# Queries and keys turned in blocks of 32 by 32 on VectorE and put in place by transfers through DRAM

## The chip, the cores and the metric

The kernel runs on one core of one Trainium2 chip. The metric is the device time of one execution in microseconds (us); the figure compared is the median of several runs. The profile is one execution taken by the hardware profiler. Its engines are PE (TensorE, with PEld for its weight loads), DVE (VectorE), ACT (ScalarE), POOL (GpSimd) and SP (SyncE, which here issues every transfer).

## What is computed

The input `x` is 8 sequences of 512 tokens with 256 features, all float32. It is normalised, and two branches read it. The first is causal attention with one head of 256 features. The second is a stack of two layers of windowed attention (8 heads of 64 features, windows of 128 tokens that also see the window before) and a gated feed-forward network. The output is `x + s * silu(g)`, with `s` from the first branch and `g` from the second.

What matters for this change is in the second branch, cut from the reference:

```python
qkv = h @ wqkv
q, k, v = jnp.split(qkv, 3, axis=-1)
q, k, v = (to_heads(q), to_heads(k), to_heads(v))
q = l2norm(q) * qs
k = l2norm(k) * ksc
q, k = rotary_xpos(q, k)
...
sim = jnp.einsum('bhwid,bhwjd->bhwij', bq, bk)
```

The product `sim` sums over the 64 features of a head. TensorE sums over partitions, so queries and keys are needed with features on partitions, while normalisation and rotation are done with tokens on partitions. Between the two, each tile of 128 tokens by 512 features has to be turned.

## The kernel before

Work is cut into slots, one for each pair of a sequence `b` and a layer `l`, in the order (0,0), (1,0), (0,1), (2,0), (1,1) and so on: 16 slots. A slot has four tiles `t` of 128 tokens; `steps` is the list of all 64 tiles. A set of generators describes the work, each yielding before a piece of TensorE work the events, buffers and PSUM banks that it needs:

- `start` loads and normalises a sequence, turns it, and runs the first branch (`qk0`, `sc0`, `pT0p`, `av0`).
- `project` multiplies a tile by the weights (`qkv`, for keys, queries and values in turn). ACT squares the result into `sq`; VectorE makes the two rotary products `r` and `side` and the sum of squares `ss`; POOL adds `side` to `r`, raises `ss` to the power -0.5 (`rn`) and multiplies `r` by it. The finished `r` is 128 tokens by 512 features.
- `turns` turns each `r`: four TensorE transposes of 128 by 128 into a PSUM bank (`qkT`), then one copy on ACT or VectorE to `qT` or `kT`, laid out as [feature within the chunk, chunk of 128 features, token].
- `all_scores` multiplies queries and keys (`sps`) on quarters of TensorE's array, 64 by 64, then masks, takes the exponent and divides. `all_turns` turns the weights (`pTp`, `pTr`), `all_sums` weighs the values (`ops`, also on quarters), and `all_outs` projects (`wop`).
- `feed_forward` does the normalisation and the network (`hps`, `hT`, `ff`, `w2p`), and `finish` the gate and the output.

`projections` keeps at most two tiles ahead of the scores. Buffers are limited by `counts`: two `qT`, three `kT`, eight `r`.

The class `Order` plans while the program is written: it keeps an account of time for TensorE, ready times of events and buffers, and a table of ranks (with the offsets in `SHIFT`) by which it chooses the next piece. TensorE executes the pieces in the order chosen. Work of VectorE, ACT and POOL is entered in each engine's own time line through `order.on`, and that fixes the order on these engines. SP is not planned: its transfers stand in the order that the framework's scheduler gives them. `STAY` is the rank by which the planner prefers to stay in the present shape of the array.

Of the kernel before, what the change touches and what calls it, by code (L numbers as in the profile page):

```python
# [14 lines left out]
P = 128  # L15
# [23 lines left out]


SHIFT = {
    "causal": {2: 1.5, 4: 1.5, 6: 1.5},
    "finish": {4: 2.75},
    "forward": {2: 1, 3: -0.5, 5: 0.25, 6: 0.75, 7: -0.25, 8: 1, 10: 1, 12: 1, 13: -0.25, 15: -0.25, 16: 1},
    "hold": {1: 4, 7: 12, 8: 12, 9: 1, 12: 24},
    "out": {4: -2, 14: 0.75},
    "project": {1: -0.25, 3: -0.5, 5: -0.5, 6: -0.5, 11: 0.5, 13: 0.75},
    "scores": {15: -2.0},
    "sum": {3: -0.75, 4: -1, 5: 0.25, 7: -0.75, 9: -0.75, 11: -0.5, 12: -0.25, 13: -0.75, 14: 1},
    "turn": {5: -0.5, 8: 0.5},  # L50
    "weigh": {0: 0.25, 2: 0.5, 3: 1, 8: 0.25, 9: 0.25, 11: 1.0, 12: -0.75, 14: 0.25},
}


# [16 lines left out]
class Order:  # L71
# [16 lines left out]
    HOLD = 2.0  # L88


    STAY = 2.0
    TURNS = 0.0

    PATIENCE = 0.0
    HOP = 0.15
    TABLE = 1.3

    LATE = {"DVE": 0.085, "ACT": 0.11, "POOL": 0.03}

    def __init__(self, tc, buffers):  # L100
        self.now = 0.0
        self.idle = 0.0
        self.shape = None
        self.changes = 0
        self.free = {tag: [0.0] * n for tag, n in buffers.items()}
        self.given = []
        self.jobs = []
        nc = tc.nc
        self.tc = tc
        self.engines = {"DVE": nc.vector, "ACT": nc.scalar, "POOL": nc.gpsimd}  # L110
        self.engines = {name: Recorder(engine) for name, engine in self.engines.items()}
        self.busy = {engine: [] for engine in self.engines}
        self.opened = {}
# [117 lines left out]
def gated_attention_kernel(  # L231
# [24 lines left out]
    dram = ctx.enter_context(tc.tile_pool(name="dram", bufs=BATCH, space=bass.MemoryType.DRAM))  # L256


    counts = {"x": 2, "xT": 4, "r": 8, "v0": 1, "oT": 1, "hn": 1, "hid": 1, "tok": 2}
    counts |= {"st": 2, "p0": 2, "p": 8, "pT": 1, "qT": 2, "kT": 3, "v": 4, "sq": 2, "side": 2}  # L260
    order = Order(tc, counts | {"bank": 8})
    vector, scalar, gpsimd = (order.engines[name] for name in ("DVE", "ACT", "POOL"))
    taken = {}

    def buffer(tag, shape, name):
        taken[name] = order.take(tag)
        return work.tile(shape, F32, tag=tag, name=name, bufs=counts[tag])

    def bank(name):
        taken[name] = order.take("bank")  # L270
        return banks.tile([P, T], F32, tag="bank", name=name)

    def free(name, at=0.0):

        order.give(taken.pop(name), at)
# [7 lines left out]
    def transpose(out, in_):  # L283
        order.took(0.11, turns=True)
        nc.tensor.transpose(out, in_, ident)  # L285
# [18 lines left out]
    def done(*key, at=0.0):  # L304
        event(*key)["at"] = max(at, order.now)
# [3 lines left out]
    arrived = {"": 3.0}  # L309

    def load(name, dst, src):
        nc.sync.dma_start(dst, src)
        arrived[""] = max(arrived[""], order.now + 2.0) + dst.free_size() * dst.shape[0] * 4 / 0.34e6
        arrived[name] = arrived[""]

    x_tiles = {}

# [122 lines left out]
    def rank(kind, i, usual):  # L440

        return usual + SHIFT.get(kind, {}).get(i, 0.0)


    def start(b):
# [125 lines left out]
        def weigh(t):  # L571
            pT, at = turned.pop(t)
            yield {"rank": rest, "at": at, "free": {"bank": 1, "st": 1}}
            av = bank(f"av0_{b}_{t}")
            for j in range(t + 1):
                matmul(av[:, 0:DIM], pT[:, j, :], v[:, j, :], j == 0, j == t)
            free(f"pT0_{b}_{t}")
            st = buffer("st", [P, DIM], f"st_{b}_{t}")
            scalar.activation(st, av[:, 0:DIM], AF.Copy, scale=rdens.pop(t))
            at = order.on("ACT", 0.47, opens="st")  # L580
            free(f"av0_{b}_{t}", at)
            nc.sync.dma_start(s[:, t, :], st)
            free(f"st_{b}_{t}", max(at, arrived[""]) + 3.0)

        yield from scores(0)
        yield from scores(1)
# [81 lines left out]
            done("projected", len(turning))  # L668
            turning.append((b, l, t, n, r, at))

    def turns():

        for i in range(2 * len(steps)):
            yield {"after": [event("projected", i)]}
            b, l, t, n, r, at = turning[i]
            nm = f"{b}_{l}_{t}"
            tag = "kT" if n else "qT"
            slot = slots.index((b, l))
            yield {"rank": rank("turn", slot, slot), "at": at, "free": {"bank": 1, tag: 1}, "turns": True}
            dst = buffer(tag, [P, IC, P], f"{tag}_{nm}")  # L680
            (kTs if n else qTs)[b, l, t] = dst
            tps = bank(f"qkT_{nm}_{n}").rearrange("p (a b) -> p a b", a=IC)
            for c in range(IC):
                transpose(tps[:, c, :], r[:, c * P : (c + 1) * P])
            at = evacuate(dst, tps, tag)
            free(f"qkT_{nm}_{n}", at)
            free(f"r_{nm}_{n}")
            done(tag, b, l, t, at=at)

    steps = [(b, l, t) for b, l in slots for t in range(NT)]  # L690
# [25 lines left out]
    def all_scores():  # L716
# [4 lines left out]
        for slot, b, l, t in pieces():  # L721
# [7 lines left out]
            for g in range(2):  # L729
# [9 lines left out]
                done("attend", b, l, t)  # L739
                qT, kT, before = qTs[b, l, t], kTs[b, l, t], kTs.get((b, l, t - 1))  # L740
                sps = [bank(f"sps_{nm}_{g}_{a}") for a in range(2)]
                whole = slice(0, P)
                blocks = [(main, ((before or kT, whole), (kT, whole)))]
                if t > 0:
                    blocks.append((rest, ((kT, low), (before, up))))
                for columns, keys in blocks:
                    for i in range(2):
                        c = 2 * g + i
                        for a, rows in enumerate(halves):
                            for queries, (tile_, some) in zip(halves, keys):  # L750
                                matmul(
                                    sps[a][queries, columns[i]],
                                    qT[rows, c, queries],
                                    tile_[rows, c, some],
                                    True,
                                    True,
                                    "quarters",
                                )
# [324 lines left out]
    def finish(b, part, last):  # L1083
        l = DEPTH - 1

        by_halves = last and part.start > 0
        start = event("windowed" if by_halves else "fed", b, l, part.start)
        yield {"after": [start] + ([event("finished", b, 0)] if by_halves else [])}
        for t in range(part.start // P, part.stop // P, 2):
            two = slice(t, t + 2)  # L1090
            yield {"after": [event("attended", b)], "free": {"x": 1}}

            again = buffer("x", [P, 2, 2, DIM], f"again_{b}_{t}")
            for i, src in enumerate((gated[b], x_r[b])):
                nc.sync.dma_start(again[:, i], src[:, two])
            there = order.now + 4.0
            for part_of in [slice(0, P), slice(P, DIM)] if by_halves else [slice(0, DIM)]:
                nm = f"{b}_{t}_{part_of.start}"
                n = part_of.stop - part_of.start
                kind = "st" if by_halves else "tok"  # L1100
                after = [event("fed", b, l, part.start, part_of.start // P)] if by_halves else []
                yield {"after": after, "free": {"bank": 1, kind: 1}}
                yT = fed[b, l, part.start]
                yps = bank(f"yps_{nm}")[:, 0 : 2 * n].rearrange("p (a f) -> p a f", a=2)
                for a in range(2):
                    for c in range(n // P):
                        on = (part_of.start // P + c) * HALF2 + (t + a) * P
                        transpose(yps[:, a, c * P : (c + 1) * P], yT[:, on : on + P])
                g = buffer(kind, [P, 2, n], f"g_{nm}")
                scalar.activation(g, yps, AF.Silu)  # L1110
                at = order.on("ACT", 0.16 + n * 1.72e-3, 0.0, "silu", kind)
                free(f"yps_{nm}", at)
                vector.tensor_mul(g, g, again[:, 0, :, part_of])
                at = order.on("DVE", 0.15 + n * 2.11e-3, max(at, there))
                vector.tensor_add(g, g, again[:, 1, :, part_of])
                at = order.on("DVE", 0.15 + n * 2.11e-3, at)
                nc.sync.dma_start(out_r[b, :, two, part_of], g)
                free(f"g_{nm}", at + 3.0)
            free(f"again_{b}_{t}", at)
        done("finished", b, part.start)  # L1120
        if last:
            free(f"xT_{b}")
# [4 lines left out]
    order.add(0, all_sums())  # L1127
    order.add(0, all_turns())
    order.add(0, all_scores())
    order.add(0, turns())  # L1130
    order.add(0, projections())
    for i, (b, l) in enumerate(slots):
        if l == 0:
# [117 lines left out]
```

## Time and profile before

| | |
|---|---|
| Time, median of 3 runs | 1439.18 us (1438.70 to 1439.65) |
| The profiled execution's own time | 1439.44 us |
| Its span | 1437.6 us |
| PE matmuls | 11834 |
| `qkT` transposes among them | 512, 75.5 us busy, overlapping |
| copies `kT<-qkT`, `qT<-qkT` | 119 on ACT, 9 on VectorE |
| transfers on SP's queue | 32.4 MB, 6.8% of 16 engines' span |

The span runs from the first to the last event that the profile records; the execution's own time is a little longer. Busy time is the union of an engine's instructions; a mean in nanoseconds is of single instructions, which overlap on PE. "Idle before" counts the time in which an engine did nothing just before instructions of that group, and names what ended the wait. The chain of work that ended last goes back from the last instruction to what released it, step by step.

### The profile page before, as it was taken

How to read it: one execution, taken by the hardware profiler on the slowest of the kernel's cores; microseconds unless marked ns; L12 is line 12 of the kernel's file. 1: busy time of each engine (PE TensorE's matmuls, PEld its weight loads, DVE VectorE, ACT ScalarE, POOL GpSimd, SP SyncE). 2: the span in 40 equal slices, each digit the busy share in tenths (PEclk: the TensorE clock that was granted, in tenths of full speed). 3: DMA queues.
4: the chain of work that ended last, by engine and by line, in shares of the span. 5: the costliest groups of instructions: out<-in, count | busy, mean ns of one | idle time of the engine just before them, and what ended most of it. 6: DMA issues, size and time to landing. Idle time of an engine off the chain costs nothing.

```text
span 1437.6 us, 30523 instructions
## 1 busy us (share of the span) xinstructions
PE 1425.3 (99%) x11834; PEld 888.4 (62%) x11834; DVE 937.8 (65%) x3004; ACT 784.2 (55%) x2038; POOL 627.5 (44%) x651
## 2 busy tenths in 40 slices
PE   8999999999999999999999999999999999999998
PEld 4666554776555556566665666556666556646667
DVE  6678545777564676667565887457587457666744
ACT  2567434757554655565554566445576448645743
POOL 5657143664413535346433466206445056423600
PEclk9999999999999999999999999999999999999999
DMA  8300000000000100100001000010000001001001
GB/s 304 105 14 16 1 1 0 13 5 17 1 2 1 45 16 1 45 30 2 16 2 45 16 2 1 1 45 31 16 2 2 1 1 46 1 1 45 2 2 59
DMA packets 27680, 34.35 MB, mean 24 GB/s; under 512 B 3176, under 2 KB 23312, under 8 KB 27536
## 3 DMA queue, kind: packets, MB, share of 16 engines
q1 hardware_dynamic: 27536, 32.40, 6.8%
q8 instruction: 94, 1.54, 0.4%
q14 instruction: 50, 0.41, 0.1%
HBM read 24.00 MB, written 8.39 MB: 23 GB/s over the span
## 4 chain that ended last, share of the span: by engine, by line
PE 90%; POOL 3%; DVE 3%; ACT 2%; issue 1%; DMA 1%; SPq 0%; POOLq 0%; ACTq 0%; DVEq 0%
PE qkv L281 21%; PE ff L281 20%; PE w2p L281 11%; PE wop L281 7%; PE ops L281 5%; PE sps L281 5%; PE qkT L285 4%; PE pTp L285 4%; PE qk L281 3%; PE sc L281 2%; PE av L281 2%; PE v0p L281 2%; POOL r L64 2%; PE pTr L285 1%; POOL rn L64 1%; PE hps L285 1%
## 5 line engine op out<-in xcount | busy, mean ns | idle before, releaser
L281 PE MATMUL qkv<-wqkv,xT 128*128 128x512 f32 x768 | 351.6, 595 | 0.1
L64 POOL TENSOR_TENSOR r<-r,side 128x512 f32<-128x512 f32 x128 | 164.7, 1287 | 427.2 <-DVE side L64 330.0
L281 PE MATMUL ff<-hn,w 128*128 128x512 f32 (+1 forms) x680 | 282.0, 568 | 0.0
L64 ACT ACTIVATE p<-p,nmx 128x192 f32<-128x192 f32 (+1 forms) x512 | 219.5, 430 | 75.3 <-DVE nmx L64 74.5
L64 POOL TENSOR_TENSOR rn<-ss,neg_half 128x8 f32<-128x8 f32 x128 | 213.8, 1670 | 10.7
L281 PEld LDWEIGHTS qkv<-wqkv,xT 128*128 128x128 f32 x768 | 137.7, 191 | 128.5 <-issue 121.9
L281 PEld LDWEIGHTS ff<-hn,w 128*128 128x128 f32 x680 | 127.3, 190 | 131.7 <-issue 124.2
L64 DVE SCALAR_TENSOR_TENSOR hid<-ff,vec,hid 128x512 f32<-128x512 f32 (+3 forms) x119 | 84.8, 716 | 140.8 <-PE ff L281 114.3
L64 DVE TENSOR_SCALAR p<-p,rden 128x192 f32<-128x192 f32 (+1 forms) x512 | 164.6, 363 | 8.7
L281 PE MATMUL w2p<-hid,w 128*128 128x512 f32 (+3 forms) x408 | 158.7, 577 | 0.0
L64 ACT ACTIVATE hid<-ff,vec 128x512 f32<-128x512 f32 (+2 forms) x102 | 66.7, 661 | 150.5 <-PE ff L281 150.2
L64 DVE CUSTOM_DVE_ANT_0 p<-sps,mask_sb 128x192 f32<-128x192 f32 (+1 forms) x512 | 142.2, 334 | 6.1 <-PE sps L281 6.0
L64 DVE TENSOR_TENSOR r<-qkv,tables 128x512 f32<-128x512 f32 x128 | 87.7, 685 | 79.4 <-ACT sq L64 79.2
L64 POOL TENSOR_TENSOR r<-r,rn 128x512 f32<-128x512 f32 x128 | 133.7, 1045 | 10.0
L64 ACT ACTIVATE sq<-qkv 128x512 f32<-128x512 f32 x128 | 75.1, 595 | 86.5 <-PE qkv L281 81.9
L281 PEld LDWEIGHTS w2p<-hid,w 128*128 128x128 f32 (+1 forms) x408 | 68.6, 189 | 78.5 <-issue 76.1
L281 PE MATMUL wop<-oT,wo 128*128 128x256 f32 x512 | 116.4, 380 | 0.0
L281 PEld LDWEIGHTS wop<-oT,wo 128*128 128x128 f32 x512 | 95.9, 190 | 18.2 <-issue 3.3
L64 POOL TENSOR_SCALAR rstd_h<-mv_h 128x2 f32<-128x2 f32 x32 | 7.5, 235 | 221.3 <-DVE mv_h L64 220.0
L281 PEld LDWEIGHTS ops<-pT,v 64*64 64x64 f32 x3584 | 82.4, 134 | 26.2 <-issue 15.6
L64 ACT ACTIVATION_READ_ACCUMULATOR p<-p,nmx 128x1 f32 x512 | 95.9, 187 | 0.0
L281 PE MATMUL sps<-kT,qT 64*64 64x128 f32 (+1 forms) x3584 | 93.4, 249 | 0.0
(92 smaller groups left out, 2105.8 us busy)
## 6 DMA issues: line engine op xcount, KB each, us to landing
s<-st SPq DMA_DIRECT2D x32, 128.0 KB, 1.8
again<-s SPq DMA_DIRECT2D x16, 256.0 KB, 3.5
again<-in_x_dram SPq DMA_DIRECT2D x16, 256.0 KB, 4.1
w<-in_w_dram SPq DMA_DIRECT2D x6, 640.0 KB, 9.5
out_dram<-g SPq DMA_DIRECT2D x15, 256.0 KB, 2.9
x<-in_x_dram SPq DMA_DIRECT2D x7, 512.0 KB, 4.7
wqkv<-in_wqkv_dram SPq DMA_DIRECT2D x2, 1536.0 KB, 10.2
tables<-in_xpos_dram SPq DMA_DIRECT2D x2, 512.0 KB, 7.5
```

The source lines that it names most:

```text
L64: ins = getattr(self.engine, name)(*args, **kwargs)
L281: nc.tensor.matmul(out, lhsT=lhsT, rhs=rhs, start=start, stop=stop)
L285: nc.tensor.transpose(out, in_, ident)
```

## The change

The function `turns` is replaced by two. `turns_out` has VectorE transpose each `r` in blocks of 32 by 32 into a buffer `rt`: inside each group of 32 partitions, 16 blocks of 32 columns are turned where they stand. Four stores, one for each group of 32 partitions (32 tokens), write `rt` to a DRAM tile `away` with the blocks put in their rows. `turns_in` loads the whole tile back as `kT` or `qT`. The blocks of a key tile lie as [group of 32 tokens, chunk, token in the group]; those of a query tile have the chunk innermost, so that in `qT` the tokens of one chunk are four elements apart. `all_scores` reads the two in these layouts; the keys of a half tile are two groups of 32.

SP gets a time line in the planner as well, so that its transfers stand in planned order. `r` has six buffers instead of eight, and `rt` two. The planner's `STAY` goes from 2.0 to 0.5, `PATIENCE` from 0 to 0.2, the kind `turn` leaves `SHIFT`, and `SHIFT` has other values.

```diff
 SHIFT = {
-    "causal": {2: 1.5, 4: 1.5, 6: 1.5},
...
+    "causal": {1: 0.75, 3: -0.5},
...
-    STAY = 2.0
+    STAY = 0.5
...
-    PATIENCE = 0.0
+    PATIENCE = 0.2
...
-    LATE = {"DVE": 0.085, "ACT": 0.11, "POOL": 0.03}
+    LATE = {"DVE": 0.085, "ACT": 0.11, "POOL": 0.03, "SP": 0.0}
...
-    counts = {"x": 2, "xT": 4, "r": 8, "v0": 1, "oT": 1, "hn": 1, "hid": 1, "tok": 2}
+    counts = {"x": 2, "xT": 4, "r": 6, "rt": 2, "v0": 1, "oT": 1, "hn": 1, "hid": 1, "tok": 2}
...
+    def send(dst, src, after, us):
+
+        sync.dma_start(dst, src)
+        return order.on("SP", 0.05, after) + us
...
-    def turns():
+    def turns_out():
...
         for i in range(2 * len(steps)):
             yield {"after": [event("projected", i)]}
             b, l, t, n, r, at = turning[i]
-            nm = f"{b}_{l}_{t}"
+            nm = f"{b}_{l}_{t}_{n}"
+            yield {"at": at - 1.0, "free": {"rt": 1}}
+            rt = buffer("rt", [P, INNER], f"rt_{nm}")
+            turned = rt.rearrange("p (g c b) -> p c g b" if n else "p (g b c) -> p c g b", c=IC, g=4)
+            vector.transpose(turned, r.rearrange("p (c g a) -> p c g a", c=IC, g=4))
+            at = order.on("DVE", 0.75, at, opens="rt")
+            free(f"r_{nm}", at)
+            away = dram.tile([P, INNER], F32, tag="turn", name=f"away_{nm}", bufs=8)
+            rows = away.rearrange("(g a) (s n) -> s a g n", g=4, s=4)
+            for s in range(4):
+                mine = rt[s * 32 : (s + 1) * 32].rearrange("a (g n) -> a g n", g=4)
+                there = send(rows[s], mine, at, 2.4)
+            free(f"rt_{nm}", there)
+            parked[b, l, t, n] = away, there
+            done("parked", i)
+
+    parked = {}
+
+    def turns_in():
+        for i in range(2 * len(steps)):
+            yield {"after": [event("parked", i)]}
+            b, l, t, n = turning[i][0:4]
+            away, at = parked.pop((b, l, t, n))
             tag = "kT" if n else "qT"
-            slot = slots.index((b, l))
-            yield {"rank": rank("turn", slot, slot), "at": at, "free": {"bank": 1, tag: 1}, "turns": True}
-            dst = buffer(tag, [P, IC, P], f"{tag}_{nm}")
-            (kTs if n else qTs)[b, l, t] = dst
-            tps = bank(f"qkT_{nm}_{n}").rearrange("p (a b) -> p a b", a=IC)
-            for c in range(IC):
-                transpose(tps[:, c, :], r[:, c * P : (c + 1) * P])
-            at = evacuate(dst, tps, tag)
-            free(f"qkT_{nm}_{n}", at)
-            free(f"r_{nm}_{n}")
+            yield {"at": at - 1.0, "free": {tag: 1}}
+            dst = buffer(tag, [P, INNER], f"{tag}_{b}_{l}_{t}")
+            at = send(dst, away, at, 2.9)
+            if n:
+                kTs[b, l, t] = dst.rearrange("p (s c b) -> p s c b", s=4, c=IC)
+            else:
+                qTs[b, l, t] = dst.rearrange("p (h n c) -> p h c n", h=2, c=IC)
             done(tag, b, l, t, at=at)
...
-                whole = slice(0, P)
-                blocks = [(main, ((before or kT, whole), (kT, whole)))]
+                blocks = [(main, ((before or kT, slice(0, 4)), (kT, slice(0, 4))))]
                 if t > 0:
-                    blocks.append((rest, ((kT, low), (before, up))))
+                    blocks.append((rest, ((kT, slice(0, 2)), (before, slice(2, 4)))))
...
                                 matmul(
-                                    sps[a][queries, columns[i]],
-                                    qT[rows, c, queries],
-                                    tile_[rows, c, some],
+                                    sps[a][halves[h], columns[i]],
+                                    qT[rows, h, c],
+                                    tile_[rows, some, c],
                                     True,
                                     True,
                                     "quarters",
```

The other transfers of the program (loads, the stores of `s`, the `again` loads and the output) are issued through `send` or `load` in SP's time line, with no change in what they move.

More of the change, by code (lines that the diff above doesn't have):

```diff
@@ L41 @@
 SHIFT = {
-    "causal": {2: 1.5, 4: 1.5, 6: 1.5},
[L43 to L51, printed above, removed]
+    "causal": {1: 0.75, 3: -0.5},
+    "finish": {6: -1.5},
+    "forward": {0: 1.5, 1: 1, 2: 0.75, 3: 1, 4: 1.5, 5: 1, 6: 0.75, 7: 1, 8: 0.75, 9: 0.75, 10: 0.75, 11: 0.75, 12: 1, 13: 2},
+    "hold": {1: 1, 3: -3, 5: 3, 7: 3, 10: 3, 11: 2, 14: 4, 15: -2.0},
+    "scores": {0: -0.75, 1: -2, 3: 0.5, 4: -1.5, 6: -1.5, 8: -1.5, 9: 0.5, 10: -1.5, 12: -1.5, 14: -2, 15: -0.75},
+    "start": {4: 1.5, 5: 1, 6: 0.75, 7: 0.75},
+    "sum": {0: 0.75, 1: 0.75, 2: 0.75, 3: -1, 6: 0.75, 8: 0.75, 9: 0.5, 10: 0.75, 12: 0.75, 14: 0.75},
+    "weigh": {3: -0.75, 5: -0.75, 8: -1.5, 10: -1.5, 11: -2},
 }
@@ L109, in __init__ @@
         self.tc = tc
-        self.engines = {"DVE": nc.vector, "ACT": nc.scalar, "POOL": nc.gpsimd}
+        self.engines = {"DVE": nc.vector, "ACT": nc.scalar, "POOL": nc.gpsimd, "SP": nc.sync}
         self.engines = {name: Recorder(engine) for name, engine in self.engines.items()}
@@ L262, in gated_attention_kernel @@
     vector, scalar, gpsimd = (order.engines[name] for name in ("DVE", "ACT", "POOL"))
+    sync = order.engines["SP"]
     taken = {}
@@ L311, in load @@
     def load(name, dst, src):
-        nc.sync.dma_start(dst, src)
+        sync.dma_start(dst, src)
+        order.on("SP", 0.05)
         arrived[""] = max(arrived[""], order.now + 2.0) + dst.free_size() * dst.shape[0] * 4 / 0.34e6
         arrived[name] = arrived[""]
+    def send(dst, src, after, us):
+        sync.dma_start(dst, src)
+        return order.on("SP", 0.05, after) + us
     x_tiles = {}
@@ L581, in weigh @@
             free(f"av0_{b}_{t}", at)
-            nc.sync.dma_start(s[:, t, :], st)
-            free(f"st_{b}_{t}", max(at, arrived[""]) + 3.0)
+            free(f"st_{b}_{t}", send(s[:, t, :], st, at, 2.0))
         yield from scores(0)
@@ L749, in all_scores @@
                         for a, rows in enumerate(halves):
-                            for queries, (tile_, some) in zip(halves, keys):
+                            for h, (tile_, some) in enumerate(keys):
                                 matmul(
-                                    sps[a][queries, columns[i]],
-                                    qT[rows, c, queries],
-                                    tile_[rows, c, some],
+                                    sps[a][halves[h], columns[i]],
+                                    qT[rows, h, c],
+                                    tile_[rows, some, c],
                                     True,
@@ L1094, in finish @@
             for i, src in enumerate((gated[b], x_r[b])):
-                nc.sync.dma_start(again[:, i], src[:, two])
-            there = order.now + 4.0
+                there = send(again[:, i], src[:, two], 0.0, 3.5)
             for part_of in [slice(0, P), slice(P, DIM)] if by_halves else [slice(0, DIM)]:
@@ L1116, in finish @@
                 at = order.on("DVE", 0.15 + n * 2.11e-3, at)
-                nc.sync.dma_start(out_r[b, :, two, part_of], g)
-                free(f"g_{nm}", at + 3.0)
+                free(f"g_{nm}", send(out_r[b, :, two, part_of], g, at, 2.5))
             free(f"again_{b}_{t}", at)
@@ L1129, in gated_attention_kernel @@
     order.add(0, all_scores())
-    order.add(0, turns())
+    order.add(0, turns_in())
+    order.add(0, turns_out())
     order.add(0, projections())
```

## Prediction

> **What bounds the kernel now.** I read the page's busy shares first, then its chain that ended last, then the windows at the two ends, and last the chain in order of time inside a steady stretch.
>
> ```profile
> PE 1425.3 (99%) x11834; PEld 888.4 (62%) x11834; DVE 937.8 (65%) x3004; ACT 784.2 (55%) x2038; POOL 627.5 (44%) x651
> ...
> PE 90%; POOL 3%; DVE 3%; ACT 2%; issue 1%; DMA 1%; SPq 0%; POOLq 0%; ACTq 0%; DVEq 0%
> ```
>
> ```profile
> 0.00:50.00 50.00, 45.14 (x181) 25.59 (x182) 33.49 (x106) 19.62 (x49) 31.36 (x47) 1.00 0.85 292
> 50.00:1350.00 1300.00, 1297.07 (x11017) 804.09 (x11016) 859.92 (x2777) 724.67 (x1903) 585.91 (x592) 1.00 0.04 14
> 1350.00:1437.60 87.60, 83.11 (x638) 58.74 (x636) 44.37 (x124) 39.87 (x89) 10.24 (x12) 0.99 0.08 25
> ```
>
> The columns after the length are busy time of PE, PEld, DVE, ACT and POOL. TensorE is idle 4.9 us in the first 50 us, 2.9 in the next 1300 and 4.5 at the end. So anything taken out of TensorE's queue in the middle shortens the span, as long as its next instruction is ready. What the removed work costs there is not its busy time (matmuls overlap) but the step from one start to the next, which the chain in time shows:
>
> ```profile
> 641.61 1.66 POOL rn L64
> 643.27 0.07 issue
> 643.34 1.05 POOL r L64
> 644.39 0.04 issue
> 644.44 0.66 PE qkT L285 x4
> 645.10 1.72 PE qkv L281 x4
> 646.82 1.50 PE ops L281 x64
> 648.31 1.34 PE sps L281 x64
> 649.65 0.37 PE pTp L285 x2
> ```
>
> ```profile
> 629.76 0.44 PE qkT L285 x4
> ```
>
> Four queued transposes take 0.44 us (0.66 where the first waits for its pipe). Sixty-four records on quarters of the array take 1.34 us when they follow others of that shape; the first block after full-array work takes 1.50, and the first two transposes after it 0.37 where a pair elsewhere takes 0.22. A visit to quarters therefore costs 0.16 + 0.15 = 0.31 us.
>
> **What the skill says.** (1) "TensorEngine Tiling (Array Packing)", Key Properties: a change of tiling mode drains TensorE. The trace agrees: 0.31 us a visit. (2) "DMA: Bandwidth & Descriptors", Anatomy of one DMA: about 2 us of a transfer are fixed, mostly until the last write is confirmed, and a wait on a semaphore is done by the issuing sequencer. The trace agrees: the stores of 128 KB land in 1.8 us. (3) "SBUF — State Buffer", Specifications: SBUF lines are 16 bytes, at least two hits per line are needed for full bandwidth, and each crossing pays. No instruction in this trace reads float32 at a stride of four, so nothing here tests it. (4) The page "VectorE: DVE Perf Modes", Rules for kernel authors, calls VectorE's transpose the fastest for 32 by 32 blocks.
>
> **The change, part by part.**
>
> *Removed from TensorE.* 128 groups of four transposes (`qkT`, 512), 0.44 us each: **-56.3 us**. The changed program's TensorE queue has none left. The evacuations go too: 119 copies on ACT at 0.585 us (70 us) and 9 on VectorE at 0.69 (6 us). They free those engines and one PSUM bank for a while; at 55% and 65% busy neither sets the end, so I count nothing.
>
> *TensorE's order.* The planner's settings changed with it. Following the built program's TensorE queue, visits to the quarters shape rise from 73 to 98: 25 x 0.31 = **+7.8 us**. All other groups of matmuls have the same number and size.
>
> *Added to VectorE.* 128 transposes of 128x512 float32. None is in the trace; the nearest rows are the products at 685 ns and the sum `ss` at 675 ns, one element a cycle. Bounds: from below 0.36, what a scaling of only 192 elements takes; from above 1.3 for the queries, should writes at a stride of 16 bytes go at half rate. I take 0.69: 128 x 0.69 = 88 us, less 16 evacuations that leave VectorE (about 11): 938 + 77 = 1015 us, 73% of the new span; with the upper value for queries, 1054. Not a bound, so no time. But a transpose now waits on VectorE for POOL's `r` and for one of two `rt` buffers, which the stores of two turns earlier must have left. Behind it in VectorE's queue stand maskings (`p<-sps`) and PSUM work, for which TensorE waits. Today that wait is TensorE's own and sums to 0.7 us in three cases, so I give it none beyond the start.
>
> *Added to SP.* Each turn issues four stores of 64 KB and one load of 256 KB: 640 more issues (119 before). Issues take 0.32 us for a store and 0.32 to 0.45 for a load: 128 x 1.7 = 218 us of SP, 16%. Moved bytes rise by 67 MB, to 99 MB or some 71 GB/s, where the start of this trace runs at 292: no bound. In SP's queue a load of `kT` waits for its four stores, and the gated stores, the `again` loads and the output stand behind it; the latter have time.
>
> *Latency from projection to scores.* Before: POOL's last `r`, 0.44 to 0.66 on TensorE, a 0.59 copy: 1.2 us. After: 0.69 on VectorE, three more issues (1.0), 1.8 to land, 0.4 to issue the load and about 3 to land (128 KB takes 1.8, `again<-s` with 256 KB 3.5 beside another): **6.9 us**. Where keys and queries are projected back to back, the chain above has the query's second projection ending at 633.66 and POOL done at 644.39: 10.7 us. Together 17.6 us, against 12.9 where POOL is free. Pricing the changed TensorE order with this trace's steps gives the work between a tile's query projection and its first score: 15.0 us at least, 26 in the median. Only three of 64 are under 17.6 (15.0, 15.3, 16.8). The deficits sum to about 5.5 us, of which 2.3 are the first tile. So **+3 us** away from the start.
>
> *The start.* In SP's changed queue all loads of layer 1 (4.7 MB) stand behind the first query's load and ahead of the second tile's stores; before, they began at 22.6 us. The first query can be stored at about 37 us and back at 42. The loads then take 13 to 16 us at 300 to 360 GB/s, to about 57; the second tile's stores, then key and query loads, land near 64. TensorE reaches that tile's scores after 51 us of work plus 7 of idle, at 58. The first tile loses 2, this one 6: **+8 us**, from 2 (another order of landing) to 15 (VectorE also blocked on `rt`).
>
> *Reads of the turned tiles.* Keys are read in runs of 32 elements; I count nothing. Queries become the stationary operand at a stride of four float32. Weight loads of 64 columns take 134 ns, of 128 columns 191, so 57 ns per 64 columns. A block of 64 records loads 16 times in each quarter: 0.91 us, hidden in 1.34. Up to 1.47 times slower costs nothing. At half rate the 48 later tiles take 1.82 instead of 1.34: +23 us; the 16 first tiles just fit. I take zero and keep 23 for the range.
>
> Sum: -56.3 + 7.8 + 3 + 8 = -37.5. From the profiled span 1437.6: 1400.1. That execution took 1439.44, 1.84 more than its span, and stands 0.26 above the median; so 1402 us.
>
> **Rivals.** (A, likeliest, 0.68) The above: 1384 if only the 56 count, 1415 with a bad start.
>
> (B) The strided weight load becomes the bound in the scores. For: the skill's 16-byte lines, and weight loads already as long as the block. Against: 0.43 us of slack in it, and the slower shape has no witness. At twice the load time, 1425. It decides against the change from 37 us on: (1.34 + 0.77) / 0.91 = 2.3 times. At four times, a later tile takes 3.65 us and a first one 1.8 where 0.9 is needed: 48 x 2.31 + 16 x 0.9 = 125 us, **1527, slower**. Slower with chance 0.06; slower only than the forecast, 0.07.
>
> (C) The round trip is not covered. If POOL or SP's queue stretch 17.6 to 20 us, 13 tiles are short by 27 us in all: 1424; at 22, 57 us and 1453. For: SP and VectorE are now in one loop with POOL and stall in order. Against: a median of 26 us. Slower 0.06, near 1424 0.12.
>
> That the change does not do what it says is out: the transposes are gone from TensorE's queue and the stores and loads are on SP's.
>
> **How the numbers follow.** Cases A, mild B and mild C are faster: 0.87. Strong B and strong C: 0.12 slower. Almost no case lands within 0.2%, which is about what a measurement can tell from no change here: 0.01. The range runs from 1386, just above all 56 us kept, to 1428, which takes in half-rate loads and 20 us of latency; strong B, strong C and a little below are left out.
>
> **What would show it.** Right: 512 fewer PE matmuls; no `qkT`; blocks of `sps` still 1.34 us in the chain; VectorE's `rt` near 0.69; TensorE idle over 10 us between 40 and 75 us and about 3 later; 7.8 us more in changes of shape. Wrong: `sps` blocks longer than 1.5 us when they follow `ops` (B); TensorE waiting for DMA into `kT` or `qT` in many windows after 100 us, or for VectorE behind `rt` (C); `rt` over 1.3 us.

## The result, and the profile after

| | before | after |
|---|---|---|
| Median of 6 runs each | 1439.18 us (1438.70 to 1439.65) | 1445.15 us (1443.91 to 1448.98) |
| Ratio, 95% interval | | 1.0045 [1.0032, 1.0058] |
| Span of the profiled execution | 1437.6 us | 1445.1 us |

The changed kernel is slower by 6.0 us, where 37 us less were predicted. The profiled execution's own time was 1447.04 us. TensorE did less work, as intended, and still ended later. From the page after: the busy shares, TensorE's granted clock in 40 slices of 36 us, and the engines of the chain that ended last.

```profile
PE 1415.4 (98%) x11322; PEld 867.2 (60%) x11322; DVE 1013.0 (70%) x3131; ACT 778.6 (54%) x1954; POOL 624.5 (43%) x651
...
PEclk9899999999999999999999999999999999999999
...
PE 89%; DMA 4%; DVE 3%; ACT 1%; SPq 1%; issue 1%; POOL 0%; DVEq 0%; ACTq 0%
```

There are 512 fewer matmuls. VectorE's 1013 us come close to the 1015 that were forecast, but by luck (see the point on VectorE below). TensorE is busy only 9.9 us less. Its idle time is the span less that: 12.3 us before, 29.7 after, and transfers now stand in the chain with 4%. The windows say where it idles (columns after the length: busy PE, PEld, DVE, ACT, POOL, then clock, DMA share, GB/s).

```profile
0.00:50.00 50.00, 40.62 (x122) 22.05 (x123) 28.65 (x80) 13.63 (x27) 23.09 (x39) 0.90 0.62 200
50.00:100.00 50.00, 44.35 (x385) 29.50 (x384) 35.34 (x117) 22.61 (x73) 29.96 (x28) 0.93 0.53 152
100.00:150.00 50.00, 48.93 (x436) 31.63 (x435) 41.90 (x129) 24.77 (x75) 32.28 (x35) 1.00 0.27 69
150.00:1350.00 1200.00, 1190.97 (x9645) 720.59 (x9647) 850.30 (x2625) 667.86 (x1658) 520.69 (x530) 1.00 0.24 62
```

TensorE idles 16.1 us in the first 150 us (4.9 before), and 9.0 from there to 1350 (2.9 before). The clock dips only in the start; a finer cut of the same view finds four such slices:

```profile
30.00:40.00 10.00, 5.61 (x20) 3.47 (x20) 6.80 (x19) 2.93 (x5) 6.97 (x9) 0.68 0.06 12
40.00:50.00 10.00, 9.49 (x30) 5.45 (x29) 3.14 (x9) 3.80 (x9) 0.00 (x0) 0.81 0.48 120
...
70.00:80.00 10.00, 4.49 (x69) 3.33 (x68) 5.60 (x16) 1.03 (x5) 5.66 (x5) 0.73 0.54 135
80.00:90.00 10.00, 10.00 (x44) 7.47 (x45) 7.08 (x28) 6.22 (x20) 2.41 (x3) 0.93 0.13 28
```

If work stretches as the granted share shrinks, the busy time in these slices holds 5.61 x 0.32 + 9.49 x 0.19 + 4.49 x 0.27 + 10.00 x 0.07 = 5.5 us more than the same work at full clock; this is an estimate. The Trainium skill ("TensorE: Matmul & The Clock Gate", What's actually happening) says that the clock is released by recent activity. The dips here fit that: they follow gaps of 1.9, 2.1 and 5.5 us and outlast them, since the slice from 80 to 90 us is busy throughout and still reads 0.93. Not every gap of that length brings a dip, as experiments 11 and 12 show.

The rest is in the scores. From the chain in time after, a block of 64 records on quarters that follows another such block:

```profile
92.07 1.50 PE ops L280 x64
93.57 1.91 PE sps L280 x64
```

The second line was 1.34 in the kernel before. `ops`, on quarters too, kept its 1.50. The records of the tile `sps` (duration min/median/max, first and last start), first before, then after:

```profile
L281 PEld LDWEIGHTS sps<-kT,qT x3584: 128/134/136, 45.0 to 1370.7; 64*64 64x64 f32 x200
```

```profile
L280 PEld LDWEIGHTS sps<-kT,qT x3584: 188/208/227, 53.8 to 1392.6; 64*64 64x64 f32 x200
...
L280 PE MATMUL sps<-kT,qT x3584: 224/280/485, 53.8 to 1392.7; 64*64 64x128 f32 x114, 64*64 64x64 f32 x86
```

The matmuls, which read the keys in runs of 32, have hardly changed (median 280 ns, 269 before). The loads of the queries, four elements apart, went from 134 to 208 ns. And VectorE's transpose is no 0.69 either for queries, whose blocks it writes four elements apart (from the groups of instructions; the mean mixes 0.70 for keys and 1.10 for queries):

```profile
L62 DVE STREAM_TRANSPOSE rt<-r 128x512 f32<-128x512 f32 x128 | 116.5, 910 | 26.5 <-POOL r L62 18.5
```

The round trip itself, in a stretch where TensorE did wait for it:

```profile
601.84 0.63 DVE rt L62
...
603.82 1.76 DMA away<-rt
...
607.47 2.44 DMA away<-rt
...
609.99 2.88 DMA qT<-away
...
613.01 2.14 PE sps L280 x64
```

The key's turn begins at 601.84 and its stores land at 605.59. In SP's queue the key's load, which waits for them, stands ahead of the query's stores; these land at 609.92, and the query is back at 612.87. Such a chain is rarely in the way, as TensorE's waits show (sum, times, longest):

```profile
PE sps L280 <- DMA qT<-away: 10.6, 5, 5.5
PE xTp L284 <- issue: 4.0, 2, 2.1
```

One wait of 5.5 us is at 71 to 77 us, in the start. The two waits of `xTp`, near 30 and 36 us, end without a releaser that the profile can name ("issue").

### The profile page after: what moved, and what is told of

Same layout as the page of the kernel before. It is cut to its first block, busy times and chain, and to the rows that moved or that the text cites. A ratio compares the mean times of both kernels' runs of the same rounds, so it can differ in the third digit from the quotient of the medians.

```text
span 1445.1 us, 30575 instructions
## 1 busy us (share of the span) xinstructions
PE 1415.4 (98%) x11322; PEld 867.2 (60%) x11322; DVE 1013.0 (70%) x3131; ACT 778.6 (54%) x1954; POOL 624.5 (43%) x651
## 4 chain that ended last, share of the span: by engine, by line
PE 89%; DMA 4%; DVE 3%; ACT 1%; SPq 1%; issue 1%; POOL 0%; DVEq 0%; ACTq 0%
PE qkv L280 21%; PE ff L280 20%; PE w2p L280 11%; PE sps L280 8%; PE wop L280 7%; PE ops L280 5%; PE pTp L284 4%; PE qk L280 3%; PE av L280 2%; PE sc L280 2%; PE v0p L280 2%; PE pTr L284 1%; SPq L62 1%; DMA away<-rt 1%; DMA qT<-away 1%
## 5 line engine op out<-in xcount | busy, mean ns | idle before, releaser
L280 PE MATMUL ff<-hn,w 128*128 128x512 f32 (+1 forms) x680 | 286.9, 569 | 0.5 <-ACT hn L62 0.4
L62 DVE TENSOR_SCALAR p<-p,rden 128x192 f32<-128x192 f32 (+1 forms) x512 | 145.9, 328 | 8.9
L280 PEld LDWEIGHTS sps<-kT,qT 64*64 64x64 f32 x3584 | 114.9, 207 | 38.2 <-issue 25.2
L62 DVE STREAM_TRANSPOSE rt<-r 128x512 f32<-128x512 f32 x128 | 116.5, 910 | 26.5 <-POOL r L62 18.5
L280 PE MATMUL sps<-kT,qT 64*64 64x128 f32 (+1 forms) x3584 | 124.4, 285 | 10.6 <-DMA qT<-away 10.6
```

Source lines behind the costliest of these rows:

```text
L62: ins = getattr(self.engine, name)(*args, **kwargs)
L280: nc.tensor.matmul(out, lhsT=lhsT, rhs=rhs, start=start, stop=stop)
```

## The experiments

The theory after this profile: the stationary operand read at a stride of four floats costs some 0.57 us a block, 48 x 0.57 = 27 us for later tiles and 3 to 4 for first ones, and the start costs some 17. Rivals: VectorE's slower turn of queries, the wait for transfers, the keys in runs of 32. Each ratio below is to the kernel before, timed anew beside that run; a difference to the kernel after is one between medians that were not taken side by side, and is good to a microsecond or two.

**1. Scores read 64 neighbouring elements.** On the kernel after; this kernel leaves out the right pairing of queries and keys, and only its time counts:

```diff
-                qTs[b, l, t] = dst.rearrange("p (h n c) -> p h c n", h=2, c=IC)
+                qTs[b, l, t] = dst.rearrange("p (h c n) -> p h c n", h=2, c=IC)
```

> The changed kernel with one edit: the scores read the 64 queries of a half tile from 64 neighbouring elements of qT instead of from elements four apart. Transfers, VectorE's work and all orders stay; the queries that meet the keys are other elements of the same tile, so the scores' values are left out of the comparison. Theory S (the strided weight load sets the pace of the scores): weight loads of sps back to 134 ns from 208, blocks of 64 records back to 1.39 us from 1.97, 48 x 0.58 + 16 x 0.2 = 31 us less, about 1414 us. Rival L (the longer way from projection to scores, with its waits, holds TensorE back): no change, 1445 us within 3.

Measured: 1418.54 us (1418.07 to 1419.73), ratio to before 0.9853 [0.9836, 0.9871], so 26.6 us less than after. The tile's loads are back:

```profile
L280 PEld LDWEIGHTS sps<-kT,qT x3584: 129/133/227, 52.8 to 1363.9; 64*64 64x64 f32 x200
```

TensorE's busy time fell by 29.5 us (1415.4 to 1385.9), while VectorE's turns and the transfers stayed as they were. A block of 64 behind `ops` takes 1.34 us again, so the keys, still in runs of 32, cost nothing that shows. The stride of the read alone turns a gain of some 21 us into a loss of 6. The time lies 4 us above the 1414 expected.

**2. VectorE writes the queries in runs of 32 too.** On top of 1, with the same left out, the keys' pattern for both:

```diff
-            turned = rt.rearrange("p (g c b) -> p c g b" if n else "p (g b c) -> p c g b", c=IC, g=4)
+            turned = rt.rearrange("p (g c b) -> p c g b", c=IC, g=4)
```

> The kernel of read_run with VectorE also writing the turned queries in runs of 32 elements instead of four elements apart (values of the scores left out as there). Theory S: the 64 transposes of queries fall from 1.10 to 0.69 us, 26 us less on VectorE, which does not set the end: within 3 us of read_run. Rival V (VectorE is the bound behind TensorE by now): another 10 us or more.

Measured: 1416.88 us (1414.78 to 1420.04), 0.9841 [0.9821, 0.9861]. All turns now take 704 ns. The interval overlaps that of 1: VectorE's 0.4 us for each of 64 query tiles bought at most a microsecond or two. It is off the path.

**3. The stride alone, in the kernel before.** ACT's copy writes `qT` with the chunk innermost, and the scores read it so:

```diff
+            if n == 0:
+                dst = dst.rearrange("p a b -> p (a b)").rearrange("p (n c) -> p c n", c=IC)
+                (kTs if n else qTs)[b, l, t] = dst
```

> The kernel before, with one edit: the copy that empties the bank of a turned query tile writes it with the four chunks innermost, so that the scores' stationary operand is read four elements apart, as in the changed kernel. TensorE's transposes, the orders and the transfers stay. Theory S: 28 to 31 us more, 1467 to 1470 us, weight loads of sps at 208 ns. Rival L: no change, 1439 us, or a few us more if the strided copies are late.

Measured: 1465.24 us (1464.93 to 1465.77), 1.0176 [1.0160, 1.0191]: 25.6 us more, with none of the rest of the change. The tile's loads, then the chain:

```profile
L281 PEld LDWEIGHTS sps<-kT,qT x3584: 188/206/215, 45.2 to 1397.0; 64*64 64x64 f32 x200
```

```profile
621.05 1.50 PE ops L281 x64
622.54 1.91 PE sps L281 x64
```

Loads and blocks are those of the kernel after. ACT now writes the queries four elements apart too, at 1100 ns a copy, but no wait for that shows: TensorE idles 10.8 us in all, 12.3 before. Runs 1 and 3 take the stride out on one side and put it in on the other, and agree within a microsecond or two.

**4. Two elements apart, in the kernel before.** As 3, but with two chunks interleaved instead of four, so that one chunk's elements are 8 bytes apart:

```diff
+                dst = dst.rearrange("p a b -> p (a b)").rearrange("p (d n e) -> p d e n", d=2, e=2)
...
-                                    qT[rows, c, queries],
+                                    qT[rows, c // 2, c % 2, queries],
```

> The kernel before with the query tile written so that the scores' stationary operand is read two elements (8 bytes) apart; everything else as before. If the penalty is one per 16-byte line that yields a single element, two elements per line are free and the time is that of before, 1439 us within 2, weight loads at 134 ns. If it grows with the stride, half of before_stride4's 26 us: about 1452 us and loads near 170 ns.

Measured: 1439.23 us, 1.0006 [0.9997, 1.0014]. It is free:

```profile
L281 PEld LDWEIGHTS sps<-kT,qT x3584: 132/135/140, 44.3 to 1370.3; 64*64 64x64 f32 x200
```

So the price sets in above 8 bytes and by 16. This fits what the Trainium skill's sentence in "SBUF — State Buffer", Specifications, says: lines of 16 bytes, two hits per line for full bandwidth. At 8 bytes there are two, at 16 one.

**5. The moving operand four apart, in the kernel before.** As 3 with `n == 1`, the keys.

> The kernel before with the key tile, the moving operand of the scores, written and read four elements apart; queries as before. If every read of TensorE pays for single elements per line: blocks of 64 records grow by about as much as with strided queries, 1460 to 1470 us. If only the weight path pays: 1439 us within 3.

Measured: 1517.09 us (1516.85 to 1517.65), 1.0547 [1.0529, 1.0564], 78 us more and far above both times expected. The matmuls of the tile and one block, of whose 64 records the trace kept 57:

```profile
L281 PE MATMUL sps<-kT,qT x3584: 290/402/420, 44.8 to 1448.5; 64*64 64x128 f32 x113, 64*64 64x64 f32 x87
```

```profile
644.22 2.77 PE sps L281 x57
```

Here no slack hides anything: a block doubles (1.34 before), against 1.4 times for the stationary operand.

**6. The start, spread by the plan.** On the kernel after, the loads of layer 1 became planned work, one group behind each of the first tiles, and sequences 2 and 3 wait for the first branch of sequence 0 (only this second edit is printed):

```diff
-        yield {"free": {"x": 1, "xT": 1} if b else {"xT": 1}}
+        yield {"after": [event("attended", 0)] if b in (2, 3) else [], "free": {"x": 1, "xT": 1} if b else {"xT": 1}}
```

> The changed kernel with the start alone changed: the loads of layer 1 are issued one or two at a time, one group for each of the first tiles, instead of all before the second tile's stores, and sequences 2 and 3 are loaded and turned only after the first branch of sequence 0. The plan of the first 200 us moves with it. Theory S with a start loss of about 18 us beside it: 8 to 15 us less, 1430 to 1437 us, and TensorE idle under 9 us in the first 100 us (15 now). Rival: the start's idle time is made up later, since later tiles have slack: under 3 us.

Measured: 1537.58 us, 1.0673 [1.0648, 1.0698]. A miss that tells nothing of the loads. TensorE's window from 50 to 100 us did fill, from 44.35 to 49.83 us busy, but the two edits changed the planner's whole order, and from 150 to 1350 us TensorE idled 71 us. The ranks and offsets were chosen for another order, and disturbing it cost far more here than what was to be measured.

**7. The start, in SP's queue alone.** The same loads kept in place in the plan but entered later in SP's time line, so TensorE's planned order stays:

```diff
-        order.on("SP", 0.05)
+        order.on("SP", 0.05, later[0])
+        later[0] += later[1]
...
+            later[:] = [order.now, 8.0]
```

(The last line stands ahead of layer 1's loads and gives each 8 us more; layer 0's last weights are entered for 24 us, behind the loads of sequences 2 and 3.)

> The changed kernel with the order of SP's queue alone changed in the first 130 us, all other queues instruction for instruction the same: sequences 2 and 3 are loaded ahead of layer 0's feed-forward weights, and layer 1's loads are spread over the next tiles' transfers. If the start costs about 17 us more than before because of that queue, most of it comes back: 1430 to 1436 us, TensorE idle under 8 us in the first 100 us. If it is TensorE's changed order there: under 4 us.

Measured: 1438.63 us (1437.66 to 1439.72), 1.0000 [0.9991, 1.0008]: 6.5 us less than after. This lies between the two times expected, and TensorE's idle time in the first 100 us, 15.0 us after, is 9.2, where under 8 was expected. The window and the waits that were 44.35 and 10.6:

```profile
50.00:100.00 50.00, 49.72 (x411) 32.66 (x410) 40.97 (x133) 27.66 (x86) 29.72 (x28) 1.00 0.48 139
```

```profile
PE sps L280 <- DMA qT<-away: 3.3, 3, 1.6
```

The order of SP's queue explains the start's second half (50 to 100 us) and its dip of the clock at 70 us. The first 50 us hardly change, 41.08 us busy against 40.62, so of the two groups of loads that moved, layer 1's, which follow, are the likely cause; they were not moved alone.

**8. A layout whose stride is free.** On the kernel after, queries lie two elements apart. VectorE turns them into that order, and two loads of 128 KB in pieces of 256 bytes replace one of 256 KB:

```diff
+                turned = rt.rearrange("p (g d b e) -> p d e g b", d=2, e=2, g=4)
...
+                to = dst.rearrange("p (d s f) -> p d s f", d=2, s=4)
+                src = away.rearrange("p (s d f) -> p d s f", d=2, s=4)
+                at = max(send(to[:, i], src[:, i], at, 2.9) for i in range(2))
...
-                                    qT[rows, h, c],
+                                    qT[rows, h, c // 2, c % 2],
```

> The changed kernel with the turned queries two elements apart: VectorE writes each block as pairs of chunks, and two loads of 128 KB (pieces of 256 bytes) put the two pairs in place; the rest and all orders of the other engines stay. Computes the whole reference. Theory S with stride 2 free: 26 to 28 us less than the changed kernel, 1417 us within 4. Rival L (two smaller loads with more pieces land later and TensorE waits): 1420 to 1440 us, with waits for qT above 15 us in all.

Measured: 1417.52 us (1416.50 to 1418.98), 0.9850 [0.9837, 0.9864], 27.6 us less than after. VectorE's turns take 706 ns, for queries too, and TensorE waits 7.1 us in all for `qT`, so rival L is out. Another layout, with VectorE's runs of 32 put in place by one load in pieces of 128 bytes, was planned and has no result.

**9. Both.** Edits 7 and 8 together.

> queries_two_loads with SP's order of start_queue_only. If the two costs are apart, both come off: 26 plus 6.5 us below the changed kernel, 1411 us within 4, faster than the kernel before by about 2%. If the faster scores only move the wait elsewhere: above 1417 us.

Measured: 1412.73 us (1411.47 to 1413.55), 0.9815 [0.9802, 0.9829]. The two gains add up to within 2 us (27.6 + 6.5 = 34.1; measured 32.4).

**10. Sequences 2 and 3 turned later.** On the kernel of experiment 9 (kernel 9 below), to free TensorE in the first 50 us, their transposes get a planned start:

```diff
-        yield {"at": at, "free": {"bank": 2}}
+        yield {"at": max(at, {2: 40.0, 3: 60.0}.get(b, 0.0)), "free": {"bank": 2}}
```

> queries_two_loads_start with the transposes of sequences 2 and 3 kept back in TensorE's plan until 40 and 60 us, so that the first branch of sequence 0 stands before them as in the kernel before; computes the whole reference. After the queue fix TensorE still runs 10 us later at the first output projection than the kernel before. If that is TensorE's changed order at 30 to 42 us (two waits of about 2 us and slow clock after them): 5 to 9 us less, about 1405 us. If it is the longer round trip of the first tile: less than 2 us.

Measured: 1414.33 us (1413.19 to 1415.85), 0.9832 [0.9819, 0.9845]: no gain, a miss. The trace says why: with the transposes gone TensorE stands near the same place, for something else. From its timeline (start, length, engine, operation; in brackets the idle time before and what ended it):

```profile
36.33 0.70 DVE L62 STREAM_TRANSPOSE rt<-r 128x512 f32<-128x512 f32 x1
...
37.13 0.27 ACT L62 COPY pT<-pT0p 128x128 f32<-128x128 f32 x1 [6.82 <-DVE rt L62]
...
37.45 1.22 PE L280 MATMUL av<-v,pT 128*128 128x256 f32 x2 [7.65 <-ACT pT L62]
```

The turned weights of the first branch take a buffer of `r`. Of six, four hold the branch's rotated tiles and two the first key and query, so ACT's copy waits until VectorE has turned that key. POOL had finished it at 29.60, but VectorE's queue held the normalisation of sequences 2 and 3 first, to 36.3. No run gave `r` a seventh buffer.

**11 and 12. That normalisation later.** On kernel 9, the same two sequences are held ahead of it, at 34 and 70 us in one kernel, at 30 and 34 in the other:

```diff
+        if b in (2, 3):
+            yield {"at": {2: 34.0, 3: 70.0}[b]}
         for t in range(0, NT, NT if b else NT // 2):
```

> Edit to queries_two_loads_start: VectorE's normalisation of sequences 2 and 3 is given a planned start of 34 and 70 us, so that VectorE turns the first key before it and the sixth buffer of r comes free for the first branch. Theory (VectorE's queue holds that buffer): TensorE's wait of 7.7 us near 30 us (as in start_order_too) falls below 2.5 us, TensorE's idle time in the first 50 us falls from 10.3 to 4 to 6.5 us, and if the rest of the plan does not get worse the time is 1405 to 1410, 3 to 8 us under 1412.7. Rival (the wait is for something else: POOL's r or the six buffers as such): idle time in the first 50 us stays above 9 us and the time is 1411 to 1416.

> As start_norms_late, with planned starts of 30 and 34 us: the first key's turn also stands ahead of the normalisation of both sequences, but the plan behind it differs. Theory: the same fall of TensorE's idle time in the first 50 us, to 4 to 6.5 us; time 1405 to 1411. Rival: idle time there above 9 us, time 1411 to 1416. If the idle time falls and the time does not, the moved plan gives it back later, and the windows after 100 us show where.

Measured: 1410.73 us (1408.19 to 1411.38), 0.9798 [0.9784, 0.9811], and 1409.68 us (1407.55 to 1410.83), 0.9794 [0.9781, 0.9807]. From the first one's timeline:

```profile
30.59 0.70 DVE L62 STREAM_TRANSPOSE rt<-r 128x512 f32<-128x512 f32 x1
```

```profile
31.70 0.70 PE L280 MATMUL av<-v,pT 128*128 128x256 f32 x2 [1.93 <-ACT pT L62]
```

The key is turned six microseconds earlier than in experiment 10 and the wait falls from 7.65 to 1.93 us, as the theory had it. TensorE's idle time in the first 50 us falls from 10.3 in kernel 9 to 6.5 and 6.4. Both are at the upper end of what was expected, and the first kernel's time lies just outside the 1405 to 1410 named. Of the idle time saved, the second kernel gives most back in the next window:

```profile
0.00:50.00 50.00, 43.56 (x162) 23.87 (x163) 29.99 (x79) 14.33 (x30) 29.71 (x45) 1.00 0.65 213
50.00:100.00 50.00, 45.66 (x499) 30.84 (x497) 41.48 (x147) 28.36 (x89) 29.63 (x31) 1.00 0.47 133
```

Idle over the whole span of the second kernel is 22.8 us against 23.7 in kernel 9; but TensorE's busy time is 4.4 us less (1382.7 against 1387.1), with the clock at 1.00 in the first window where it was 0.90. So the second kernel's gain seems to have come mostly with the clock, which the theory did not have. The first kernel has the same wait of 1.93 us near 30 us as the second, and reads 0.66 from 30 to 40 us where the second reads 1.00. The gain over kernel 9 is 2 to 3 us, with intervals that just overlap. These two are the fastest of all, 28 and 29 us below the kernel before.

## Why the prediction was wrong, point by point

**The failed step: "Queries become the stationary operand at a stride of four float32 ... I take zero."** The slack was reckoned well: 0.91 us of loads in a block of 1.34, free up to 1.47 times. The loads went past it. A block of 64 has 16 loads in each quarter; 1.91 / 16 = 119 ns each, if they set it, against 57: 2.1 times. That is near the bound called half rate, priced at 23 us; it measured 25.6 to 27.6 on whole kernels (experiments 3, 1 and 8) and some 31 by blocks. Of the 43 us between the forecast of 1402 and the 1445 measured, most is this one term. The text named the 16-byte lines and the sign (blocks over 1.5 us after `ops`), had no row of the trace for the case, and took the cheap end.

**Rival B** put the turning point at 37 us, or 2.3 times the load time, with every other term as forecast. The cost stayed below that, and the change lost all the same because of the next term.

**The start: +8 predicted, some +17 measured** (11.2 us more idle before 150 us, and the 5.5 estimated for the lower clock). Experiment 7 shows that 6.5 us of this are the order of SP's queue; the cause named, layer 1's loads ahead of the second tile's stores, is the likely part of that order. Of the rest, experiments 11 and 12 won back 2 to 3 us. SP's queue in the trace after:

```profile
44.48 1.78 SPq L62 DMA_DIRECT2D away<-rt  x4
...
50.95 0.43 SPq L62 DMA_DIRECT2D sc<-in_qk_scale_dram  x1
...
65.09 7.00 SPq L62 DMA_DIRECT2D away<-rt  x8
```

The first query was stored at 44.5 us, not at 37; behind its load stood a store of the first branch, issued at 50.6, so layer 1's loads began at 51, not 42, and ended at 70, not 57. What made it late was not in the forecast: the order of VectorE's queue held TensorE near 30 us. In this kernel the two gaps stand before the transposes `xTp` of sequences 2 and 3, whose `x` VectorE scaled only from 31.73 and 34.94 us on. With these transposes moved, six buffers of `r` and the same order of VectorE's queue held TensorE instead (experiments 10 to 12). The prediction asked who waits behind VectorE's turn, but not who waits for the buffer that it frees. The lower clock was left out as well.

**The removed transposes: -56.3, and the visits: +7.8.** Their counts stand: no `qkT` is left, and the traces show 73 visits before and 98 after. Their prices were not measured apart, but the sum comes near. TensorE's busy time should change by -56.3 + 7.8 + 31 (48 blocks at 0.57, 16 half blocks at about 0.2) + 5.5 = -12.0; it changed by -9.9. Idle time adds 17.4, for +5.4 in all against a span longer by 7.5. The 2.1 us between are not placed.

**The round trip: +3 away from the start.** From 150 to 1350 us TensorE idles 6.1 us more than before, 4.1 of it waiting for `qT`. The 6.9 us reckoned are near the usual case: from SP's timeline, with 2.7 us for a load to land, the 64 queries take an estimated 7.5 in the median. Some take longer, as in the stretch shown, 9.9 from the start of the query's turn to its scores, since SP waits for the key's stores ahead of issuing the query's. Rival C is out: of 10.6 us waited for `qT`, 5.5 are one wait in the start, and the other four waits sum to 5.1. The section behind the forecast's point (2), on the fixed 2 us, describes transfers that GpSimd issues; those here are SP's, and the 1.8 us that the forecast used are the trace's own.

**VectorE: 0.69 for a turn.** Right for keys (0.70), wrong for queries (1.10, between the bounds given), and with no clear effect, as experiment 2 shows. The total came out by luck: the turns keep VectorE busy for 116.5 us, not 88, but other work shrank by more than the 11 us forecast, `p<-p,rden` alone from 164.6 to 145.9 us for a reason that is open. No run compares this transpose of 32 by 32 blocks with another of such blocks, so the forecast's point (4) stays untested. The freed copies of ACT brought nothing that shows, as said, and ACT is hardly freer: its busy time fell from 784.2 to 778.6 us, not by 70, mainly since 104 loads of function tables stand where 61 stood (78.3 us):

```profile
L62 ACT ACT_TABLE_LOAD x104 | 133.4, 1283 | 2.8 <-PEq L1264 0.7
```

In sum: -37.5 predicted, +31 for the scores, +9 for the start and +3 for other waits give about the +5.4 above. In the forecast's list, the transposes alone would give 1439.2 - 56.3 = 1383, not 1384; nothing rests on it. Without the stride (experiment 8) the change is worth 21 to 22 us, and with the start mended as well up to 29.

## What to carry to other kernels

When a change moves data into a new layout, price each reader and writer at its new stride first; here 16 bytes cost TensorE about half of what the removed transposes gave, while 8 bytes, reached with the same transposes and one more load, cost nothing. Where a trace has no row for the new access, do not take the cheap end because slack seems to cover it: a slack of 1.47 is thin against a plausible doubling. And when work moves to another engine's queue, follow the buffers that it now frees, since the next to wait may be on neither engine.

## What the runs showed of the hardware

- Weight loads of 64 columns of float32: 134 ns with neighbouring elements, 135 at 8 bytes apart, 206 to 208 at 16. Moving operand of up to 128 columns: 269 ns, and 402 at 16 bytes.
- Writes pay too. VectorE's transpose of 128x512: 0.70 us, 1.10 with elements 16 bytes apart, 0.71 at 8. ACT's copy of the same size from PSUM, in experiments 3 and 4: 586 ns, 636 at 8 bytes and 1100 at 16 (medians). From the groups of instructions of experiment 3, with the mean:

```profile
L64 ACT COPY qT<-qkT 128x512 f32<-128x512 f32 x63 | 69.3, 1100 | 28.0 <-PE qkT L285 27.9
```

- In the kernel after, idle gaps of 1.9 and 2.1 us near 30 and 36 us went with a granted clock of 0.68 in that slice and 0.81 in the next, where TensorE was busy 95% of the time. So a gap can be paid for twice, but need not be: one of 1.9 us at the same place went with 0.66 in the first kernel of experiments 11 and 12 and with 1.00 in the second. What decides it is open.
